# Banks, order and gates in the end phase of a perceiver layer

## The chip, the cores and the metric

The kernel runs on one core of one Trainium2 chip. The time is the device time of the whole program in microseconds, the median of several executions. The program has 70,354 instructions in the profile before.

## The reference, cut to what matters

There are 16 sequences of 128 rows and 512 columns, and each of the three parts adds its result to x:

```python
x = x + xattn(layernorm(x), ctx)      # 16 heads, 2048 context rows for each sequence
x = x + attn(layernorm(x))            # a state-space layer, then an MLP, see below
x = x + ffn(layernorm(x))

# attn, for Z = layernorm(x):
Z_mam = rmsnorm(mamba(Z) + Z) * norm1_w            # in_proj, conv, scan over 128 steps, out_proj
h     = gelu(Z_mam @ mlp_w1.T + mlp_b1)            # 512 -> 2048, the "first matrix"
mlp   = h @ mlp_w2.T + mlp_b2                      # 2048 -> 512, the "second matrix"
attn  = rmsnorm(mlp + Z_mam) * norm1_w

# ffn, for xf = layernorm(x):
scores = softmax(xf @ W_gate)                      # 7 columns, the "gate"
w      = top-2 of scores, divided by their sum
ffn    = xf @ W_shared.T + (sum of w) * (xf @ W_expert.T) + bias   # no token is over capacity here
```

All is in fp32.

## The kernel before

**Stages.** The program is written out in steps u = 0 to 313, in an order set by hand; each engine executes its own instructions strictly in that order and waits for the others by semaphores. For u below 256 (NU, "live") attention fills TensorE. The scan of the state-space layer follows 54 steps behind: each step has two halves, each with ScalarE's decays (L656), VectorE's scan (L670) and product with C (L673) and GpSimd's products and sums (L635, L686). The scan's data bc come by DMA two loads a step (L584).

**The end phase** begins at u = 256, at about 3130 us. Attention's memory is given up and the pool `ffn` opened. The 16 sequences now pass in 8 pairs m = 0 to 7 (i = 0, 1 in a pair) through the MLP and the last part, while the scans of the last sequences still run (until about 3705 us). The work is cut into units, each a list of loads, of TensorE calls, of calls that follow (`post`) and of extra loads. `feed(k)` issues the loads of unit k+2, the extra loads of unit k+1, the post calls of unit k-1 and then the TensorE calls of unit k. Units are dealt out evenly over the steps u; those left after the last step follow without a pause. A pair has:

- four `hidden` units (L829): quarter q of the first matrix, 2 x 16 profile records of 256 columns into two PSUM banks; post: `gelus` (ScalarE, L843, between two table loads), which reads both banks. With quarter 3 go the transposes of the pair before (`x_turned`, L802, and VectorE's copies fT, L813);
- two `expert` units of the pair before (L960): for each sequence 8 records with wex and 8 with wsh, 512 columns each, into a bank each. The first has the `gate` of both sequences ahead (L917, 16 records of 7 columns, one bank). Post: `gated` (softmax and top two, a chain of small VectorE operations, L931 to L951) and `result` (L973 with pe of wex, L976 with psh of wsh, then the output transfer, L977);
- four `second` units (L859): 16 records each, into two banks (`accs`) that are held over all four; post of the last: `mlp_sum` (L877 and moments), and in the next pair's first two quarters `mlp_norm` (L890, L893) and `last_norm` (L906 makes xf; GpSimd adds fbias, L909).

Records: a matmul of fp32 is two records in the profile, each with its own weight load (PEld).

**Banks.** PSUM has eight banks of 512 columns: banks[0] to [3], avp, pa, hst and pc. In the end phase hst and pc hold the scan. `bank()` deals out banks[0], banks[1], avp and pa in a ring of four; each hidden unit 0 of a pair skips two. banks[2] and banks[3] serve the late work of the state-space layer alone: its in_proj (`x_part` and `z_part`, L518, read by ScalarE L528 and VectorE L533), dt (L602, read by ScalarE L606 and VectorE L609), x_proj (L572), the products that turn and scale attention's results (L451, L464, L511) and out_proj (`projected`, L699, read by VectorE L708). The names in the profile: `bank` is any of banks[0] to [3].

**Loads.** All of the loads named here go through SyncE's queue (SP) in program order: weights `wf` (L763, L766; 6 buffers, that is three units), bc (L584), wout (L496), `xr` (L780, the pair's rows, 4 buffers) and x1 (L785).

**The last pair.** Pair 7 has `turn_unit`, its four hidden units, the experts of pair 6, its four second units, and then in one list, for each i: `mlp_sum`, `mlp_norm`, `last_norm`; and for each i: `x_turned`, `gate`, `experts`, `gated`, `result`.

Of the kernel before, what the change touches and what calls it, by code (L numbers as in the profile page):

```python
# [8 lines left out]
FP = mybir.dt.float32  # L9
# [6 lines left out]
P = 128  # L16
# [18 lines left out]
def perceiver_layer(ctx: ExitStack, tc: tile.TileContext, a: dict, out: bass.AP):  # L35
# [28 lines left out]
    def moments(pool, dst, src):  # L64
        st = pool.tile([P, 6], FP, tag="st", name="st", bufs=4)
        nc.vector.bn_stats(st, src)
        nc.vector.bn_aggr(dst, st)
# [41 lines left out]
    with ExitStack() as es:  # L109
# [31 lines left out]
        def heads(ps):  # L141
            return ps.rearrange("p (k q) -> p k q", q=P)
# [572 lines left out]


        fpool, fcs, xrs, hss, mTs, fTs, accs, stage, done = [], {}, {}, {}, {}, {}, {}, {}, set()
        wfs, turn_of = {}, [0]

        def open_ffn():  # L720
            p = es.enter_context(tc.tile_pool(name="ffn", bufs=1))
# [24 lines left out]
        def flat(ps):  # L746
            return ps.rearrange("p k q -> p (k q)")

        def bank():
            t = (banks[0], banks[1], flat(avp), flat(pa))[turn_of[0] % 4]  # L750
            turn_of[0] += 1
            return t

        def seqs(m):
            return [(i, m * MB + i) for i in range(MB)]
# [17 lines left out]
        def load_z(m):  # L773
            for i, b in seqs(m):
                assert b in done
                if m:
                    xrs[b] = fpool[0].tile([P, D], FP, tag="xr", name=f"xr{b}", bufs=4)
                else:
                    xrs[b] = keep.tile([P, D], FP, tag="x", name=f"xr{b}", bufs=4)
                nc.sync.dma_start(xrs[b], zd[b])  # L780
# [24 lines left out]
        def x_turned(m, ii):  # L805

            for i in ii:
                b = m * MB + i
                turned_in(stage.pop((b, "xf")), b, "fT")
            for i in ii:  # L810
                b = m * MB + i
                fTs[b] = fpool[0].tile([P, KC, NQ], FP, tag=f"fT{i}", name=f"fT{b}")
                nc.vector.tensor_copy(fTs[b], heads(stage.pop((b, "fT"))))  # L813

        def turned_pair(m):
            t = fpool[0].tile([P, KC, MT], FP, tag="mT", name=f"mT{m}")
            mTs[m] = t
            for i, b in seqs(m):
                copy = nc.vector.tensor_copy if i else nc.scalar.copy
                copy(t[:, :, i * NQ : (i + 1) * NQ], heads(stage.pop((b, "mT"))))  # L820

        def hidden(m, q):
            if q == 0:
                turn_of[0] += 2
            ps = [bank(), bank()]
            for j in range(4):
                w = wfs[m, 1, q, j // 2]
                for kc in range(KC):
                    nc.tensor.matmul(  # L829
                        ps[j // 2][:, j % 2 * MT : (j % 2 + 1) * MT],  # L830
                        w[:, kc, j % 2 * P : (j % 2 + 1) * P],
                        mTs[m][:, kc, :],
                        start=(kc == 0),
                        stop=(kc == KC - 1),
                    )
            stage[m, q] = ps

        def gelus(m, q):
            ps = stage.pop((m, q))
            t = fpool[0].tile([P, 4, MT], FP, tag="hs", name=f"hs{m}_{q}", bufs=4)  # L840
            for j in range(4):
                fc = q * 4 + j
                nc.scalar.activation(  # L843
                    t[:, j, :],
                    ps[j // 2][:, j % 2 * MT : (j % 2 + 1) * MT],
                    AF.Gelu,
                    bias=fcs["b1"][:, fc : fc + 1],
                )
            nc.scalar.preload_act_table_set("natural_log_exp_and_others")
            hss[m, q] = t  # L850

        def second(m, q):
# [18 lines left out]
        def mlp_sum(m, ii):  # L871

            n = len(ii)
            mv2, r, ms = small("mv2", [P, n, 2]), small("r2", [P, n]), small("ms", [P, n])
            for j, i in enumerate(ii):
                x = xrs[m * MB + i]
                nc.vector.tensor_tensor(x, x, accs[m][i], ALU.add)  # L877
                moments(keep, mv2[:, j, :], x)
            mean_square(keep, ms, mv2)
            inv_sqrt(keep, r, ms, 1e-6)  # L880
            stage[m, *ii, "r2"] = r
# [27 lines left out]
                nc.gpsimd.tensor_tensor(xrs[b], xrs[b], fcs["fbias"], ALU.add)  # L909
                stage[b, "xf"] = xf  # L910

        def gate(m, ii):
            n = len(ii)
            ps = bank()[:, 0 : n * 8].rearrange("p (i e) -> p i e", e=8)[:, :, 0:NE]
            for j, i in enumerate(ii):
                for kc in range(KC):
                    nc.tensor.matmul(  # L917
                        ps[:, j, :],
                        fTs[m * MB + i][:, kc, :],
                        fcs["wg"][:, kc, :],  # L920
                        start=(kc == 0),
                        stop=(kc == KC - 1),
                    )
            stage[m, *ii, "g"] = ps

        def gated(m, ii):

            n, pg = len(ii), stage.pop((m, *ii, "g"))
            gm, gs = small("gm", [P, n, 1]), small("gs", [P, n, 1])
            sc, top = small("sc", [P, n, 8]), small("top", [P, n, 8])  # L930
            nc.vector.tensor_reduce(gm, pg, AX.X, ALU.max)  # L931
            nc.vector.memset(sc, 0.0)
            nc.vector.tensor_tensor(
                sc[:, :, 0:NE], pg, gm.to_broadcast([P, n, NE]), ALU.subtract
            )
            nc.scalar.activation(sc[:, :, 0:NE], sc[:, :, 0:NE], AF.Exp)
            nc.vector.tensor_reduce(gs, sc[:, :, 0:NE], AX.X, ALU.add)
            nc.vector.reciprocal(gs, gs)
            nc.vector.tensor_tensor(
                sc[:, :, 0:NE], sc[:, :, 0:NE], gs.to_broadcast([P, n, NE]), ALU.mult  # L940
            )
            for j in range(n):
                nc.vector.max(top[:, j, :], sc[:, j, :])
            nc.vector.tensor_tensor(gs, top[:, :, 0:1], top[:, :, 1:2], ALU.add)
            nc.vector.reciprocal(gs, gs)
            nc.vector.tensor_tensor(
                top[:, :, 0:2], top[:, :, 0:2], gs.to_broadcast([P, n, 2]), ALU.mult
            )


            nc.vector.tensor_tensor(gs, top[:, :, 0:1], top[:, :, 1:2], ALU.add)  # L951
            for j, i in enumerate(ii):
                stage[m * MB + i, "gs"] = gs[:, j, :]

        def experts(m, i):
            b = m * MB + i
            ps = [bank(), bank()]
            for t, w in zip(ps, (fcs["wex"], fcs["wsh"])):
                for kc in range(KC):
                    nc.tensor.matmul(  # L960
                        t,
                        fTs[b][:, kc, :],
                        w[:, kc, :],
                        start=(kc == 0),
                        stop=(kc == KC - 1),
                    )
            stage[b, "e"] = ps

        def result(m, i):
            b = m * MB + i  # L970
            pe, psh = stage.pop((b, "e"))
            r = flat_tile(f"res{b}")
            nc.vector.scalar_tensor_tensor(  # L973
                r, pe, stage.pop((b, "gs")), xrs[b], ALU.mult, ALU.add
            )
            nc.vector.tensor_tensor(r, r, psh, ALU.add)  # L976
            nc.sync.dma_start(out[b], r)  # L977


# [3 lines left out]
        def unit(loads=(), pe=(), post=()):  # L983
            units.append(([*loads], [*pe], [*post], []))
# [19 lines left out]
                units[-1][1].insert(0, call(x_turned, m - 1, both))  # L1004

        def expert_units(m):
            for i in range(MB):
                unit((), [call(experts, m, i)], [call(result, m, i)])
            units[-2][1].insert(0, call(gate, m, both))
            units[-2][2].insert(0, call(gated, m, both))  # L1010

        def second_units(m):
            for q in range(4):
# [35 lines left out]
        turn_unit(m, ())  # L1049
        units[-1][1].pop(0)  # L1050
        hidden_units(m)
        expert_units(m - 1)
        second_units(m)
        for i in both:
            units[-1][1].extend(call(f, m, (i,)) for f in (mlp_sum, mlp_norm, last_norm))
        for i in both:
            units[-1][1].extend([call(x_turned, m, (i,)), call(gate, m, (i,))])
            units[-1][1].extend([call(experts, m, i), call(gated, m, (i,)), call(result, m, i)])


        late, after, inner, middle, loads, head, behind = ({} for _ in range(7))
# [94 lines left out]
        for u in range(last):  # L1156
# [26 lines left out]
                weighted(u - 1)  # L1183
            if u == NU:
                att.close()
                open_ffn()
            if u == NU + 8:
                load_wex()
# [31 lines left out]
            for f in middle.get(u, ()):  # L1220
                f()
            for i, f in enumerate(after_turns):
                f(banks[(3 + i) % 4 if live else 2 + i % 2])
            if live and after_turns:
                turn(u, 3, (3 + len(after_turns)) % 4)
            for f in behind.get(u, ()):
                f(pc.rearrange("p k q -> p (k q)") if makes else banks[2])
            for f in after.get(u, ()):
                f()
            for f in inner.get(u, ()):  # L1230
# [81 lines left out]
```

## Time and profile before

| | |
|---|---|
| median of three runs | 3881.88 us (3880.52 to 3889.77) |
| the profiled execution | 3884.85 us |
| its span, first to last instruction | 3883.1 us |
| granted TensorE clock, mean | 0.986 |
| busy share of PE, DVE, ACT, POOL | 97%, 70%, 63%, 54% |
| PE busy in 3140 to 3724 us (584 us) | 539.0 us |
| DVE, ACT, POOL busy there | 399.8, 279.6, 370.2 us |

PE is TensorE's matmuls, PEld its weight loads, DVE VectorE, ACT ScalarE, POOL GpSimd, SP SyncE; L829 is line 829 of the kernel before. In a timeline a row gives its start, its length, the engine, line and operation, output<-inputs, shape, the number of instructions in it, and in brackets the idle time ahead of it and what ended that. In the waits a row gives who waited for whom, the sum in us, the number of waits and the longest. A row of stretches gives the stretch, its length, the busy time and count of PE, PEld, DVE, ACT and POOL, the granted TensorE clock (1.00 is full), the DMA engines' busy share and GB/s. The ends of matmuls are modelled, so their pace is read from start to start.

### The profile page before, as it was taken

How to read it: one execution, taken by the hardware profiler on the slowest of the kernel's cores; microseconds unless marked ns; L12 is line 12 of the kernel's file. 1: busy time of each engine (PE TensorE's matmuls, PEld its weight loads, DVE VectorE, ACT ScalarE, POOL GpSimd, SP SyncE). 2: the span in 40 equal slices, each digit the busy share in tenths (PEclk: the TensorE clock that was granted, in tenths of full speed). 3: DMA queues.
4: the chain of work that ended last, by engine and by line, in shares of the span. 5: the costliest groups of instructions: out<-in, count | busy, mean ns of one | idle time of the engine just before them, and what ended most of it. 6: DMA issues, size and time to landing. Idle time of an engine off the chain costs nothing.

```text
span 3883.1 us, 70354 instructions
## 1 busy us (share of the span) xinstructions
PE 3771.4 (97%) x26120; PEld 2868.8 (74%) x26120; DVE 2713.3 (70%) x4852; ACT 2445.5 (63%) x5847; POOL 2104.8 (54%) x1968
## 2 busy tenths in 40 slices
PE   7999999999999999999999999999999989899998
PEld 6888787778777877787778777877787756555654
DVE  3444445887778787878787878787878776758732
ACT  3555556777767776777677767776777654434421
POOL 1111113675667566756676657665766575657710
PEclk9999999999999999999999999999999999999999
DMA  2111122444444444444445354435353477567641
GB/s 91 42 34 44 50 71 78 139 148 136 140 161 147 144 140 159 143 149 137 161 138 157 124 167 146 152 118 177 130 162 121 153 261 237 180 230 239 227 157 59
DMA packets 341223, 548.40 MB, mean 141 GB/s; under 512 B 24432, under 2 KB 225408, under 8 KB 340624
## 3 DMA queue, kind: packets, MB, share of 16 engines
q1 hardware_dynamic: 340464, 543.28, 42.6%
q8 instruction: 206, 3.38, 0.4%
q14 instruction: 137, 1.12, 0.1%
q0 software_dynamic: 416, 0.63, 0.1%
HBM read 527.29 MB, written 16.52 MB: 140 GB/s over the span
## 4 chain that ended last, share of the span: by engine, by line
PE 81%; DVE 10%; ACT 4%; issue 2%; DMA 2%; POOL 1%; SPq 0%; DVEq 0%; ACTq 0%; POOLq 0%
PE pa L237 21%; PE pc L237 15%; PE bank L330 10%; PE bank L299 7%; PE bank L518 6%; PE avp L343 6%; PE bank L699 3%; DVE hst L670 2%; DVE nm L307 2%; PE bank L859 2%; DVE w L673 2%; PE bank L395 2%; PE bank L464 2%; PE bank L960 1%; PE bank L829 1%
## 5 line engine op out<-in xcount | busy, mean ns | idle before, releaser
L307 DVE TENSOR_REDUCE nm<-bank 128x1 f32<-128x512 f32 x1024 | 634.9, 682 | 251.3 <-PE bank L299 250.3
L686 POOL TENSOR_TENSOR ysum<-ysum,w 128x512 f32<-128x512 f32 x384 | 500.5, 1303 | 500.5 <-DVE hst L649 303.3
L317 ACT ACTIVATE pr<-bank,nm 128x512 f32<-128x512 f32 x1024 | 689.7, 687 | 95.0 <-DVE nm L307 89.2
L635 POOL TENSOR_TENSOR w<-dx,bc 128x512 f32<-128x512 f32 x512 | 649.5, 1290 | 3.8
L335 ACT COPY pT<-bank 128x512 f32<-128x512 f32 x816 | 437.6, 585 | 222.0 <-PE bank L330 217.9
L670 DVE TENSOR_TENSOR_SCAN hst<-hst,w 128x512 f32<-128x512 f32 x456 | 556.9, 1221 | 11.9 <-ACT hst L656 8.1
L656 ACT ACTIVATE hst<-dt,alog 128x254 f32<-128x254 f32 x912 | 436.4, 478 | 169.0 <-DVE hst L649 150.5
L330 PE MATMUL bank<-ident,pr 128*128 128x128 f32 x4096 | 525.4, 275 | 16.2 <-ACT pr L317 14.3
L330 PEld LDWEIGHTS bank<-ident,pr 128*128 128x128 f32 x4096 | 472.0, 142 | 74.6 <-ACT pr L317 22.2
L343 PEld LDWEIGHTS avp<-pT,v 128*32 128x32 f32 x8192 | 208.0, 109 | 193.9 <-issue 193.9
L673 DVE TENSOR_TENSOR w<-hst,bc 128x512 f32<-128x512 f32 x456 | 315.3, 692 | 47.8 <-DMA bc<-bcd 32.4
L299 PE MATMUL bank<-kt,qT 32*128 32x512 f32 x2048 | 297.7, 642 | 6.1 <-DVE avs L458 5.7
L229 POOL TENSOR_TENSOR t<-c,c 128x512 f32<-128x512 f32 x128 | 164.8, 1288 | 252.3 <-PE pc L237 244.7
L343 PE MATMUL avp<-pT,v 128*32 128x128 f32 x8192 | 276.8, 276 | 0.0
L237 PE MATMUL pa<-t,ks 128*128 128x256 f32 x1024 | 249.3, 386 | 0.0
L237 PE MATMUL pa<-vs,t 128*128 128x256 f32 x1008 | 244.7, 386 | 0.0
L518 PE MATMUL bank<-zT,win 128*128 128x256 f32 x1024 | 234.6, 383 | 4.6 <-ACT hs L843 4.6
L518 PEld LDWEIGHTS bank<-zT,win 128*128 128x128 f32 x1024 | 192.0, 192 | 30.9 <-ACT hs L843 5.0
L237 PEld LDWEIGHTS pa<-vs,t 128*128 128x128 f32 x1008 | 185.4, 190 | 34.6 <-issue 10.1
L317 ACT ACTIVATION_READ_ACCUMULATOR pr<-bank,nm 128x1 f32 x1024 | 209.6, 205 | 0.0
L237 PEld LDWEIGHTS pa<-t,ks 128*128 128x128 f32 x1024 | 185.1, 190 | 32.7 <-issue 10.3
L333 DVE COPY pT<-bank 128x512 f32<-128x512 f32 x208 | 143.8, 691 | 89.1 <-PE bank L330 86.5
(274 smaller groups left out, 6849.4 us busy)
## 6 DMA issues: line engine op xcount, KB each, us to landing
bc<-bcd SPq DMA_DIRECT2D x512, 512.0 KB, 4.3
c<-in_ctxT_dram SPq DMA_DIRECT2D x256, 256.0 KB, 4.4
wf<-in_w_dram SPq DMA_DIRECT2D x128, 512.0 KB, 7.3
wqo<-in_wqkvo_dram SPq DMA_DIRECT2D x128, 256.0 KB, 4.8
win<-in_win_dram SPq DMA_DIRECT2D x128, 256.0 KB, 4.6
wout<-in_wout_dram SPq DMA_DIRECT2D x128, 256.0 KB, 4.3
x<-in_x_dram SPq DMA_DIRECT2D x16, 256.0 KB, 3.6
x1d<-x SPq DMA_DIRECT2D x16, 256.0 KB, 2.2
```

Source lines behind the costliest of these rows:

```text
L237: nc.tensor.matmul(ps[:, r, :], l[:, kc, r * P : (r + 1) * P], m[:, kc, :], start=(i in (1, 2, 5) and r == 0 and kc == 0), stop=(r == 1 an ...
L299: nc.tensor.matmul(banks[j], qts[b][rows, hg, :], kts[u // 4, hg][rows, :], start=True, stop=True)
L307: nc.vector.tensor_reduce(stats[b][0][j][:, sb, hg : hg + 1], banks[j], AX.X, ALU.max, negate=True)
L317: nc.scalar.activation(pr[:, j, :], banks[j], AF.Exp, bias=nm[j][:, sb, hg : hg + 1], accum_out=sm[:, sb, h : h + 1],)
L330: nc.tensor.transpose(ps[:, j, :], prs[u][:, j, i * P : (i + 1) * P], ident)
L335: nc.scalar.copy(pT, ps)
L343: nc.tensor.matmul(avp[j * HD : (j + 1) * HD, hg, :], vts[u // 4, hg // 2, i // 2][:, i % 2, hg % 2 * P + j * HD : hg % 2 * P + (j + 1) * HD],
L518: nc.tensor.matmul(ps, w[:, kc, :], zTs[g][:, kc, :], start=(kc == 0), stop=(kc == KC - 1))
L635: nc.gpsimd.tensor_tensor(w, dx.unsqueeze(1).to_broadcast([P, NH // 2, GT]), bcs[g * 32 + r, 0][:, i * NH // 2 : (i + 1) * NH // 2, :], AL ...
L656: nc.scalar.activation(bt(h[:, k, :])[:, :, 1:], bt(dt)[:, :, 1:], AF.Exp, scale=aneg[:, ec, n : n + 1],)
L670: nc.vector.tensor_tensor_scan(flat, flat, w.rearrange("p n t -> p (n t)"), 0.0, ALU.mult, ALU.add)
L686: nc.gpsimd.tensor_tensor(s, s, w, ALU.add)
```

## The change

- `bank()` takes the oldest entry of a list, `free_banks`; six banks are put into it at u = 256 (pa, banks[2], banks[1], avp, and banks[3] and banks[0] after `turned_pair`), and each reader gives its bank back where it is issued. The late work takes its banks from the same list.
- `xr` has 6 buffers instead of 4.
- `gate` is gone: in `experts` each chunk's gate matmul follows the wex matmul on the same fT chunk. `gated` comes after both experts; `result` is split: first xr + psh, later, in `result_last`, + gs x pe, and the output transfer.
- For the last pair the second units, with `mlp_sum`, `mlp_norm` and `last_norm`, come ahead of the experts of pair 6; `x_turned` of each sequence of pair 7 stands after an expert unit of pair 6; then follow the two expert units of pair 7.

```diff
         def bank():
-            t = (banks[0], banks[1], flat(avp), flat(pa))[turn_of[0] % 4]
-            turn_of[0] += 1
-            return t
+            return free_banks.pop(0)
+
+        def give_back(*ps):
+            free_banks.extend(ps)
...
-                    xrs[b] = fpool[0].tile([P, D], FP, tag="xr", name=f"xr{b}", bufs=4)
+                    xrs[b] = fpool[0].tile([P, D], FP, tag="xr", name=f"xr{b}", bufs=6)
...
-                nc.vector.tensor_copy(fTs[b], heads(stage.pop((b, "fT"))))
+                ps = stage.pop((b, "fT"))
+                nc.vector.tensor_copy(fTs[b], heads(ps))
+                give_back(ps)
...
         def hidden(m, q):
-            if q == 0:
-                turn_of[0] += 2
             ps = [bank(), bank()]
...
             nc.scalar.preload_act_table_set("natural_log_exp_and_others")
+            give_back(*ps)
             hss[m, q] = t
...
                 nc.vector.tensor_tensor(x, x, accs[m][i], ALU.add)
+                give_back(accs[m][i])
...
-        def experts(m, i):
-            b = m * MB + i
+        def experts(m, ii, j):
+
+            b = m * MB + ii[j]
+            if j == 0:
+                stage[m, *ii, "g"] = bank()
+            pg = stage[m, *ii, "g"][:, j * 8 : j * 8 + NE]
             ps = [bank(), bank()]
-            for t, w in zip(ps, (fcs["wex"], fcs["wsh"])):
+            for t, w in zip(ps, ("wex", "wsh")):
                 for kc in range(KC):
-                    nc.tensor.matmul(
-                        t,
-                        fTs[b][:, kc, :],
-                        w[:, kc, :],
-                        start=(kc == 0),
-                        stop=(kc == KC - 1),
-                    )
+                    for o, x in ((t, w), (pg, "wg"))[: 2 if w == "wex" else 1]:
+                        nc.tensor.matmul(
+                            o,
+                            fTs[b][:, kc, :],
+                            fcs[x][:, kc, :],
+                            start=(kc == 0),
+                            stop=(kc == KC - 1),
+                        )
             stage[b, "e"] = ps
 
         def result(m, i):
             b = m * MB + i
-            pe, psh = stage.pop((b, "e"))
+            pe, psh = stage[b, "e"]
             r = flat_tile(f"res{b}")
-            nc.vector.scalar_tensor_tensor(
-                r, pe, stage.pop((b, "gs")), xrs[b], ALU.mult, ALU.add
-            )
-            nc.vector.tensor_tensor(r, r, psh, ALU.add)
+            nc.vector.tensor_tensor(r, xrs[b], psh, ALU.add)
+            give_back(psh)
+            stage[b, "e"] = pe, r
+
+        def result_last(m, i):
+            b = m * MB + i
+            pe, r = stage.pop((b, "e"))
+            nc.vector.scalar_tensor_tensor(r, pe, stage.pop((b, "gs")), r, ALU.mult, ALU.add)
+            give_back(pe)
             nc.sync.dma_start(out[b], r)
...
         def expert_units(m):
-            for i in range(MB):
-                unit((), [call(experts, m, i)], [call(result, m, i)])
-            units[-2][1].insert(0, call(gate, m, both))
-            units[-2][2].insert(0, call(gated, m, both))
+            for i in both:
+                unit((), [call(experts, m, both, i)], [call(result, m, i)])
+            units[-1][2].append(call(gated, m, both))
+            units[-1][2].extend(call(result_last, m, i) for i in both)
...
         hidden_units(m)
-        expert_units(m - 1)
         second_units(m)
         for i in both:
             units[-1][1].extend(call(f, m, (i,)) for f in (mlp_sum, mlp_norm, last_norm))
+        expert_units(m - 1)
+        units[-1][1].insert(0, call(x_turned, m, (0,)))
+        units[-1][1].append(call(x_turned, m, (1,)))
         for i in both:
-            units[-1][1].extend([call(x_turned, m, (i,)), call(gate, m, (i,))])
-            units[-1][1].extend([call(experts, m, i), call(gated, m, (i,)), call(result, m, i)])
+            unit(
+                (),
+                [call(experts, m, (i,), 0)],
+                [call(f, m, x) for f, x in ((gated, (i,)), (result, i), (result_last, i))],
+            )
...
             if u == NU:
                 att.close()
+                give_back(flat(pa), banks[2], banks[1], flat(avp))
                 open_ffn()
...
             for i, f in enumerate(after_turns):
-                f(banks[(3 + i) % 4 if live else 2 + i % 2])
+                ps = banks[(3 + i) % 4] if live else bank()
+                f(ps)
+                if not live:
+                    give_back(ps)
...
             for f in behind.get(u, ()):
-                f(pc.rearrange("p k q -> p (k q)") if makes else banks[2])
+                ps = flat(pc) if makes else banks[2] if live else bank()
+                f(ps)
+                if not live:
+                    give_back(ps)
```

## The prediction

> **What bounds the kernel now.** I read the page first, then the waits of PE in the end phase (3120 us to the end), then PE's timeline around the longest of them, the timeline of SP's queue, the last 40 us, and last the stretches of DVE. The page says where to look:
>
> ```profile
> PE 3771.4 (97%) x26120; PEld 2868.8 (74%) x26120; DVE 2713.3 (70%) x4852; ACT 2445.5 (63%) x5847; POOL 2104.8 (54%) x1968
> ...
> PE   7999999999999999999999999999999989899998
> ```
>
> Over the span of 3883.1 us PE is the bound, and what it loses it loses at the end: the last eight slices are the end phase, the only part that the change touches. Its waits there:
>
> ```profile
> PE bank L829 <- ACT hs L843: 12.7, 3, 4.7
> PE bank L917 <- DVE fT L813: 8.1, 2, 7.2
> PE bank L859 <- DMA wf<-in_w_dram: 6.5, 1, 6.5
> ...
> PE pa L829 <- ACT hs L843: 5.8, 1, 5.8
> PE avp L829 <- ACT hs L843: 5.4, 1, 5.4
> ```
>
> Three causes: the first matrix (L829) waiting for gelus to empty a bank, 23.9 us; a weight transfer, 6.5 us; the tail's chain (L917 and L802), 8.1 us here and 4.5 of L802. (A wait of L518 for L533's reads, 4.6 us in pair 1, stays as it is.) A wait costs more than its length. In pair 3:
>
> ```profile
> 3443.78 3.62 PE L829 MATMUL pa<-mT,wf 128*128 128x256 f32 x16
> 3447.23 0.59 PE L602 MATMUL bank<-xd,dtw 128*128 128x256 f32 x2
> 3447.66 1.28 PE L802 MATMUL bank<-ident,xf 128*128 128x128 f32 x8
> 3454.35 6.20 PE L829 MATMUL avp<-mT,wf 128*128 128x256 f32 x16 [5.41 <-ACT hs L843]
> 3460.39 3.62 PE L829 MATMUL pa<-mT,wf 128*128 128x256 f32 x16
> ```
>
> Sixteen records take 3.45 us from start to start at full clock (3443.78 to 3447.23) and 6.04 us after the wait (3454.35 to 3460.39): a wait of 5.41 us also costs 2.6 us of half clock.
>
> **Part 1, the banks.** The ring of four gives the last quarter of the first matrix the very banks of the quarter before it, because the two transposes of the other pair took the two in between. So PE waits there until gelus has read them. Such waits stand in pairs 1, 3, 4, 5 and 6: 3.83 + 5.41 + 5.81 + 4.67 + 4.16 = 23.9 us, and the matmuls behind them run 1.8, 2.6, 2.1, 2.0 and 3.1 us over their full-clock pace: 11.5 us. Together 35.4 us. With six banks in one line the order of the changed program puts that quarter into banks of the quarter before the last, of the dt product (L602), or of an x or z product; none waits for the newest gelus.
>
> What is late next? (a) The quarter's second half then reuses L602's bank in pairs 3 and 4. L602 ended at 3447.66 and DVE's read of it (L609) at 3453.02: 5.4 us. PE comes back to the bank after 0.87 us of transposes and 3.45 us of matmuls, 4.3 us: a wait of 1.1 us. (b) The first expert product takes a bank that the newest gelus must free. In pair 3 gelus ended 7.8 us after its matmuls (3455.03 against 3447.23); PE is back after 0.43 + 0.87 + 6.9 = 8.2 us: none, just. (c) In pair 1, expert product and second matrix take banks that an x product (L518) left 1.7 to 2.2 us before. L602 sits in that place now and waits 0.5 us: two such, bounds 0 to 5 us, I take 2. (d) The last projection's DVE read stands 0.9 us ahead of the second matrix of pair 6; DVE idles there (9.41 us busy in the 50 us from 3700), so 0.2 us.
>
> Against all this stands DVE:
>
> ```profile
> 3500.00:3600.00 100.00, 93.90 (x330) 60.38 (x329) 80.83 (x157) 49.86 (x105) 73.88 (x70) 0.97 0.69 236
> 3600.00:3700.00 100.00, 88.99 (x324) 59.40 (x323) 76.98 (x146) 51.50 (x102) 68.47 (x60) 0.96 0.71 242
> ```
>
> ```profile
> DVE w L673 <- DMA bc<-bcd: 11.7, 3, 5.1
> ```
>
> Two stretches of 100 us, then DVE's waits from 3500 to 3700. DVE's busy time is the third of a stretch's: 79%, and another 12% of these 200 us it waits for something other than PE (11.7 for bc, 7.6 for ACT's decays, 5 of small ones). A pair takes 82 us there (3508.79 to 3590.57 for pair 4). DVE so needs about 75 us, 70 if the DMA waits go; PE's matmuls at full clock need 73: four quarters 27.6, second matrix 27.5, experts with gates 15.4, transposes and a dt product 2.2. The removed stalls cannot all be won with the engines so close and each in order. I let 3 us a pair come back as short waits in the five pairs, 15 us; bounds 0 and, if DVE is the bound, all 35.
>
> A clock question hangs on those short waits. In this trace a wait of 3.01 us (L572 for POOL, 3344.00) was followed by half clock: four transposes took 0.91 us instead of 0.44, and in all 2.6 us were lost; waits of 1.80 us and less were not. The Trainium skill ("TensorE: Matmul & The Clock Gate", Part 1) has the clock halve only after an idle window of about 3.4 us. By the page, short waits cost their length; by the row, one of 3 us nearly doubles. If all five did, that would be 13 us more.
>
> **Part 2, six xr buffers.** SP's queue in pair 2:
>
> ```profile
> 3372.59 5.84 SPq L780 DMA_DIRECT2D xr<-zd  x2
> ...
> 3386.77 0.99 SPq L766 DMA_DIRECT2D wf<-in_w_dram  x2
> ```
>
> SP stands from 3363 on: the reload of xr waits until the results of the pair two back have been read out of its buffer (3372.57 and 3378.09), and everything behind it on SP stands too: bc, wout and the weights wf, for some 15 us. PE then waits 1.1 + 6.5 us for wf and loses another 2.9 us to half clock: the 48 records from 3372.61 plus the 1.27 us ahead of them came to 10.5 us over pace. With six buffers the owner was done a pair earlier. The weights come up to 15 us earlier than a wait of 6.5 needs: I count all 10.5 us as gone, bounds 0 and 10.5.
>
> **Part 3, gates.** Sixteen sequences times 8 records at 0.1065 us (16 in 1.70 us, 3463.84 to 3465.55) are 13.6 us in both kernels. Interleaved, the first gate record of a chunk hides its weight load behind a 512-column matmul; the second and the next expert matmul show theirs: two a chunk, eight a sequence, as now. Cost 0; bounds 13.6 less (loads skipped) and 13.6 more (each switch showing one more). No row has such a switch; the nearest, 128-column transposes, also come at 0.107 a record. The Trainium skill ("TensorE: Matmul & The Clock Gate", "Back-to-back issue gap") gives a matmul of up to 64 columns a floor of 25 ns; by that the gates would shrink by 128 x 0.08 = 10 us, an estimate from the page that enters no sum. The top-two chain and the product with pe move behind both experts; DVE does them while PE is in the second matrix, but its later result holds the gate bank and two expert banks longer, which the six banks cover.
>
> **Part 4, the tail.**
>
> ```profile
> 3841.93 3.60 PE L859 MATMUL avp<-wf,hs 128*128 128x512 f32 x8
> 3850.04 1.12 PE L802 MATMUL pa<-ident,xf 128*128 128x128 f32 x4 [4.52 <-DVE xf L906]
> 3858.34 1.87 PE L917 MATMUL bank<-wg,fT 128*128 128x7 f32 x8 [7.17 <-DVE fT L813]
> ...
> 3871.30 1.06 PE L917 MATMUL bank<-wg,fT 128*128 128x7 f32 x8 [0.94 <-DVE fT L813]
> ```
>
> From the end of the first accumulator (3841.93) to the end of the span are 41.2 us now, and pair 6's experts took another 15.5 us before the second matrix (3802.37 to 3817.89): 56.7. Changed: second accumulator 3.43; four expert blocks of 3.43 + 0.86 + 3.43 = 7.72; two transposes of 0.43; and one new wait, since the first expert block of pair 7 takes the bank of the transposes just ahead of it and must await DVE's copy, 0.94 as in the last row. That is 36.1 us. Then DVE: 0.2 + 0.69 for psh and now 0.79 for pe after it, and 3.05 us of output transfer (3880.05 to 3883.1 now). Sum 40.9; gain 15.8. DVE's two chains (3842.20 to 3857.68) end 15.7 us after that start; PE first wants their second result at 3.43 + 7.72 + 0.43 + 7.72 = 19.3 us. Cover 3.6 us; past it, each us of DVE delay costs one.
>
> The weights for the second matrix follow straight on the first's; the first matrix already streams four quarters unbroken from 3777, with loads two units ahead, and SP's order puts pair 6's output transfers behind all of them instead of between. POOL, past which pair 7's additions of fbias move, is idle from 3800.
>
> **Sum.** Banks 35.4 - 15 - 2; transfer 10.5; tail 15.8: 44.7 us off the profiled execution's 3884.85 gives 3840.2. The median of the runs, 3881.88, lies 3.0 below that execution: 3837.
>
> **Rivals.**
> (A) The stalls only change owner: DVE's 75 us and in-order queues hold the pairs, and the tail alone is won: 3881.9 - 16 = 3866. For it: 79% plus 12%. Against: DVE itself waited 11 us on late gates and 16 us on the projections between 3400 and 3700, waits that an earlier PE ends.
> (B) Nothing comes back: 35.4 + 10.5 + 15.8 = 62 off, 3820. For it: (a), (b) and (d) are each about a microsecond.
> (C) Slower: banks whose reader is DVE stand close behind their writer in the new line. If DVE trails PE so that each of six pairs waits w more, plus 2.6 us half clock, the 62 us are eaten when 6(w + 2.6) = 62, w = 7.7 us; at w = 12 it is 3908. Against: L609's 5.4 us is what DVE trails now.
> (D) No change: each gate switch shows one more weight load (13.6 us), and the stalls change owner as in (A): 3880.
>
> **Numbers.** Forecast 0.52, A 0.20, B 0.16, C 0.07, D 0.05. Range 3818 to 3868: just past B and just past A. Some 0.3%, 12 us, is what a measurement can tell from no change: faster 0.88 (forecast, A, B), same 0.05 (D), slower 0.07 (C).
>
> **What would show it.** Right: no wait of the first matrix for gelus over 2 us in pairs 3 to 6; no half clock between them; no xr reload standing on SP; PE unbroken from the second matrix of pair 7 to its last product but for about 1 us; gates at 0.21 us a chunk. Wrong: PE waits on L609 or L533 banks of over 3 us; DVE over 90% busy from 3500; PE waiting for scans at the projections; 512-column matmuls off their 0.43 us pace beside gates.

## The result, and the profile after

The changed kernel takes 3821.44 us (median; 3821.10 to 3821.82) against 3882.53 us for the kernel before, measured beside it: 61 us less, a ratio of 0.9839 with a 95% interval of 0.9822 to 0.9856. The profiled execution took 3821.10 us, its span 3819.3.

The predicted time was 3837, so 15.6 us too long. The time lies beside rival B, "nothing comes back", at 3820. All of the profile after has the line numbers of the changed kernel: the first matrix is L834 (L829 before), the second L865 (L859), transposes of x L805 (L802), their copies L817 (L813), xf L913 (L906), experts and gates L960.

The page first, its head, the line of engines and PE's slices:

```profile
span 3819.3 us, 70341 instructions
...
PE 3747.7 (98%) x26120; PEld 2856.3 (75%) x26120; DVE 2711.8 (71%) x4852; ACT 2445.3 (64%) x5847; POOL 2104.1 (55%) x1968
...
PE   7999999999999999999999999999999989999999
```

Three of the last eight slices were at 8 before, one is now, that in which the end phase begins. The waits of PE from 3120 us to the end, all that are 0.5 us or longer:

```profile
PE pa L834 <- DMA wf<-in_w_dram: 7.3, 1, 7.3
PE bank L518 <- ACT hs L848: 4.6, 1, 4.6
PE bank L834 <- issue: 3.9, 1, 3.9
PE bank L572 <- POOL xa L566: 3.0, 1, 3.0
PE avp L805 <- DVE xf L913: 2.8, 1, 2.8
PE avp L699 <- DMA wout<-in_wout_dram: 1.8, 1, 1.8
PE bank L330 <- ACT pr L317: 1.7, 4, 0.7
PE bank L960 <- DVE fT L817: 0.8, 1, 0.8
PE bank L834 <- DVE dt L609: 0.7, 1, 0.7
PE avp L602 <- ACT zs L547: 0.5, 1, 0.5
PE bank L865 <- ACT zs L547: 0.5, 1, 0.5
```

The first matrix no longer waits for a gelu anywhere (23.9 us before), the second no longer for weights (6.5), and the tail's 12.6 us of waits have become 0.8. What is left was there before, but for the line of L834 on L609 (0.7), which the prediction had at 1.1. Three waits have grown: 2.8 us for xf in pair 5 (1.8 at the same place before), 7.3 for the first weights of the phase (6.0) and 1.8 for wout (0.8). The 4.6 us of L518 are the wait for L533's reads that the prediction names: the last of these ends at 3227.53 us and L518 starts at 3227.63, while the view puts the wait down to a gelu. In pair 3, where the timeline before had a wait of 5.41 us and half clock:

```profile
3427.33 0.59 PE L602 MATMUL bank<-xd,dtw 128*128 128x256 f32 x2
3427.76 1.28 PE L805 MATMUL bank<-ident,xf 128*128 128x128 f32 x8
3428.88 3.62 PE L834 MATMUL bank<-mT,wf 128*128 128x256 f32 x16
3433.17 3.72 PE L834 MATMUL bank<-mT,wf 128*128 128x256 f32 x16 [0.67 <-DVE dt L609]
3436.73 1.02 PE L960 MATMUL avp<-wex,fT 128*128 128x512 f32 x2
```

From start to start the quarter's halves take 4.29 us with the wait and 3.56 us, against 3.45 at full pace; no gelu is waited for, and the clock stays full.

SP's queue in pair 2, in which the reload of xr stood before:

```profile
3365.83 0.49 SPq L597 DMA_DIRECT2D dtw<-in_dtproj_dram  x1
3367.04 0.95 SPq L769 DMA_DIRECT2D wf<-in_w_dram  x2
3368.39 1.03 SPq L982 DMA_DIRECT2D out_dram<-res  x2
3369.68 1.20 SPq L584 DMA_DIRECT2D bc<-bcd  x2
```

Weights, results and bc follow each other with no xr among them; pair 3's rows were loaded earlier. VectorE over the same two stretches of 100 us as before (its busy time is the third of each stretch):

```profile
3500.00:3600.00 100.00, 97.06 (x352) 62.96 (x350) 83.58 (x148) 61.12 (x122) 81.76 (x75) 0.98 0.68 227
3600.00:3700.00 100.00, 100.00 (x324) 58.35 (x323) 58.06 (x127) 33.63 (x67) 49.15 (x43) 1.00 0.69 242
```

It is busier in the first (83.6 against 80.8) and far less busy in the second (58.1 against 77.0): the scans are done sooner, the last starts at 3659.8 us and not at 3702.2. The tail:

```profile
3778.15 3.60 PE L865 MATMUL avp<-wf,hs 128*128 128x512 f32 x8
...
3797.54 0.60 PE L805 MATMUL bank<-ident,xf 128*128 128x128 f32 x4
3798.92 1.13 PE L960 MATMUL bank<-wex,fT 128*128 128x512 f32 x2 [0.78 <-DVE fT L817]
3799.89 0.28 PE L960 MATMUL pa<-wg,fT 128*128 128x7 f32 x2
3800.03 1.10 PE L960 MATMUL bank<-wex,fT 128*128 128x512 f32 x2
...
3811.03 3.68 PE L960 MATMUL bank<-wsh,fT 128*128 128x512 f32 x8
```

From the second accumulator's start (3778.15) to the end of the span are 41.15 us; the prediction's sum was 40.9.

**Where the time went.** For every TensorE record of the end phase I took the time from its start to the next one's start, less what such a record takes at full clock without a wait (0.429 us for 512 columns, 0.215 for 256, 0.1075 for 128, 0.1065 for a gate's 7). That is the time over pace: waits and half clock together. In both kernels the records at full pace come to 645 us. Over pace, in three sections: from the first matrix's first record until the second out_proj of the phase has passed (pairs 0 to 2), from there to the transposes of pair 7 (pairs 3 to 6), and from these to the end.

| profiled execution | pairs 0 to 2 | pairs 3 to 6 | pair 7 and tail |
|---|---|---|---|
| before | 40.2 | 35.2 | 24.8 |
| predicted for the change | 29 | 17 | 8 |
| changed | 19.2 | 7.0 | 8.3 |

The predicted row is the one before, less the prediction's gains by place. First section: pair 1's wait with its half clock, 5.6, and the transfer, 10.5, less 3 + 2 given back. Second: four waits of 20.1 us with 9.8 of half clock, less 4 x 3. Third: 15.8, and the 0.8 us that VectorE's later product adds behind PE's end. The two excesses of 10 us, less the 1.2 us by which the end phase began later (3134.46 against 3133.26), are the 19 us by which the profiled execution beat the sum (3821.1 against 3840.2). The tail has no part in it.

### The profile page after: what moved, and what is told of

It reads as the page before. It is cut to its first block, busy times and chain, and to the rows that moved or that the text cites. A ratio compares the mean times of both kernels' runs of the same rounds, so it can differ in the third digit from the quotient of the medians.

```text
span 3819.3 us, 70341 instructions
## 1 busy us (share of the span) xinstructions
PE 3747.7 (98%) x26120; PEld 2856.3 (75%) x26120; DVE 2711.8 (71%) x4852; ACT 2445.3 (64%) x5847; POOL 2104.1 (55%) x1968
## 4 chain that ended last, share of the span: by engine, by line
PE 84%; DVE 9%; ACT 3%; issue 2%; DMA 1%; POOL 1%; SPq 0%; DVEq 0%; ACTq 0%; POOLq 0%
PE pa L237 21%; PE pc L237 15%; PE bank L330 10%; PE bank L299 7%; PE avp L343 6%; PE bank L518 5%; PE bank L865 3%; PE bank L699 3%; DVE hst L670 2%; PE bank L834 2%; PE bank L960 2%; DVE nm L307 2%; PE bank L395 2%; DVE w L673 2%; PE bank L464 1%
## 5 line engine op out<-in xcount | busy, mean ns | idle before, releaser
L518 PE MATMUL bank<-zT,win 128*128 128x256 f32 x968 | 222.0, 383 | 4.6 <-ACT hs L848 4.6
L237 PEld LDWEIGHTS pa<-t,ks 128*128 128x128 f32 x1024 | 184.7, 190 | 32.6 <-issue 10.5
L518 PEld LDWEIGHTS bank<-zT,win 128*128 128x128 f32 x968 | 181.5, 192 | 28.7 <-ACT hs L848 5.0
```

Of the source, the lines that this page charges most:

```text
L237: nc.tensor.matmul(ps[:, r, :], l[:, kc, r * P : (r + 1) * P], m[:, kc, :], start=(i in (1, 2, 5) and r == 0 and kc == 0), stop=(r == 1 an ...
L518: nc.tensor.matmul(ps, w[:, kc, :], zTs[g][:, kc, :], start=(kc == 0), stop=(kc == KC - 1))
```

## The experiments

Theory N: the removed stalls stay away, because six xr buffers also free the data that VectorE waits for. Theory G, the prediction's: VectorE is so near its limit that some 3 us a pair come back. All kernels are compared with the kernel before, run on the same chip (medians 3880.3, 3881.2 and 3880.4 us for the three sets below).

### The parts one by one

Six xr buffers in the kernel before, nothing else:

```diff
-  xrs[b] = fpool[0].tile([P, D], FP, tag="xr", name=f"xr{b}", bufs=4)
+  xrs[b] = fpool[0].tile([P, D], FP, tag="xr", name=f"xr{b}", bufs=6)
```

> The kernel before with six xr buffers, nothing else. Both theories take the reload of xr off SP's queue in pair 2. Theory N (nothing comes back): the 10.5 us of the late weights go, 3871, and VectorE's waits for bc (11.7 us from 3500 to 3700) fall below 2 us; the waits of the first matrix on gelus stay, 24 us in all. Theory G (VectorE gives the rest back, as predicted): the same 10.5, since this term holds none of the give-back. A rival: the late weights were only hidden behind the next wait, 3876 to 3882.

Measured 3867.77 us, ratio 0.9969 (0.9957 to 0.9980): 12.5 off. The second matrix's wait for wf in pair 2 fell from 6.5 to 0.9 us. VectorE's waits for bc fell from 32.4 to 9.4 us over the end phase, and from 3500 to 3700 none is left among its waits. The waits for gelus stayed (21.5 us). The term of 10.5 us holds.

The banks alone: `bank()`, `give_back` and every place that gives a bank back as in the change, on the kernel before.

```diff
-            t = (banks[0], banks[1], flat(avp), flat(pa))[turn_of[0] % 4]
-            turn_of[0] += 1
-            return t
+            return free_banks.pop(0)
...
-            if q == 0:
-                turn_of[0] += 2
...
+            give_back(*ps)
```

> The kernel before with the six banks in one line alone: four xr buffers, gates ahead of the expert matmuls, the old order of the tail. Theory N (short waits do not come back): 35.4 us go, 3847. Theory G (3 us a pair come back as short waits, and 2 for the banks of L518): 3864. A third, theory S: the stalls do come back here, because TensorE reaches the reload of xr earlier and SP then stands longer, and only six xr buffers keep them away: 3858 or more, with waits for wf or bc of over 10 us in pairs 2 to 6.

Measured 3854.63 us, ratio 0.9934 (0.9922 to 0.9947): 25.7 off, of 35.4, by the medians 9.7 us less than the sum and between N and S. The execution that was profiled, 3848.96 us, is the fastest of the five, so its trace shows where time came back rather than how much of these 9.7 us.

The same with six xr buffers:

> The kernel before with six banks in one line and six xr buffers; gates and tail as before. Theory N: 35.4 + 10.5 = 46 us off, 3836, so that gates and tail are worth the other 15 us. Theory G: 28 off, 3853, and what the changed kernel gained beyond that came from the interleaved gates. Theory S: 3836 as N, but more than the sum of the two parts alone.

Measured 3836.05 us, ratio 0.9888 (0.9873 to 0.9903): 44.2 off, of 45.9. Now next to nothing comes back. The parts alone sum to 38.2; the 6 us between are no larger than the intervals allow by chance, so the traces must say where they are. VectorE's waits for bc from 3330 to 3690 us, in the kernel before, with the banks alone and with both:

```profile
DVE w L673 <- DMA bc<-bcd: 25.6, 7, 5.1
```

```profile
DVE w L673 <- DMA bc<-bcd: 27.4, 9, 6.3
```

```profile
DVE w L673 <- DMA bc<-bcd: 9.0, 5, 4.2
```

(0.3 us with the buffers alone, 1.4 in the changed kernel.) So four buffers keep these waits as they were, and six remove most of them, with the old banks as with the new. Where VectorE stands behind the reload, TensorE can stand behind VectorE. One such place with the banks alone, PE's timeline in pair 3:

```profile
3480.75 1.02 PE L863 MATMUL bank<-wf,hs 128*128 128x512 f32 x2
3483.61 0.65 PE L803 MATMUL pa<-ident,xr 128*128 128x128 f32 x4 [1.84 <-DVE xr L796]
3484.27 1.06 PE L803 MATMUL bank<-ident,xr 128*128 128x128 f32 x4
3485.13 4.92 PE L863 MATMUL avp<-wf,hs 128*128 128x512 f32 x8
```

The wait for the next pair's rows (z_norm, which VectorE reaches late) costs 2.0 us and, with the half clock until 3487.8, another 2.0 (1.3 of it in the last row). The sections, over pace, in one execution each:

| profiled execution | pairs 0 to 2 | pairs 3 to 6 | pair 7 and tail |
|---|---|---|---|
| before, 3884.85 us | 40.2 | 35.2 | 24.8 |
| buffers alone, 3867.92 us | 28.3 | 29.2 | 24.2 |
| banks alone, 3848.96 us | 27.8 | 12.8 | 23.0 |
| both, 3835.92 us | 20.9 | 4.7 | 24.6 |

The 29.9 us of stalls removed in pairs 3 to 6 would leave 5.3 of the 35.2: so 7.5 came back without the buffers and none with them. But the buffers alone took 6.0 us off these pairs, where the prediction counted nothing for them (among them shorter gelu waits, 5.17 us instead of 5.81 in pair 4 and 2.35 instead of 4.16 in pair 6). There the parts alone sum to 6.0 + 22.4 = 28.4 us and both took 30.5: most of it is what each is worth by itself, and that one helps the other beyond this, by 2 us here and 6 by the medians, is not shown beyond the noise.

The new order of the last pair alone, on the kernel before (gates apart, the ring of four banks):

```diff
         hidden_units(m)
-        expert_units(m - 1)
         second_units(m)
...
+        expert_units(m - 1)
+        units[-1][1].insert(0, call(x_turned, m, (0,)))
+        units[-1][1].append(call(x_turned, m, (1,)))
```

> The kernel before with the new order of the last pair alone: pair 7's second matrix ahead of pair 6's experts, its transposes around the second of these; old ring of banks, four xr buffers, gates ahead of the experts. Both theories: 15.8 us off, 3866, and TensorE's waits for L906 and L813 after 3800 fall from 12.6 us to about 1. If the ring of four makes the experts wait for banks: 3868 to 3872.

Measured 3870.61 us (3866.08 to 3876.23), ratio 0.9976 (0.9968 to 0.9985): 9.7 off, not 15.8. The ring is why, in PE's timeline:

```profile
3834.26 0.60 PE L802 MATMUL bank<-ident,xf 128*128 128x128 f32 x4
3838.30 6.59 PE L960 MATMUL avp<-wex,fT 128*128 128x512 f32 x8 [3.44 <-DVE sc L933]
```

The second expert block gets the bank in which pair 6's gates lie, and VectorE reaches these only behind pair 7's two norms: 3.4 us of wait and 3.0 of half clock. On top of banks and buffers the same order, with the interleaved gates, took the span from 3834.1 to 3819.3 us: 14.8. So the tail's gain needs the six banks, which the prediction had not seen.

### The gates

The changed kernel with the gate records as a block ahead of the expert records of each sequence:

```diff
-            for t, w in zip(ps, ("wex", "wsh")):
+            for t, w in zip((pg, *ps), ("wg", "wex", "wsh")):
```

> The changed kernel with the 8 gate records of a sequence ahead of its 16 expert records, as a block, instead of one after each chunk of wex. Prediction's term (cost 0): 3821, within 2 us. If interleaving saved weight loads or issue gaps: up to 13.6 us slower, 3835. If each switch between gate and expert chunk cost something: up to 13.6 us faster, 3808. A place where it can cost by another way: the tail's two last blocks, where the gate's results come 3 us earlier here, which is off the path that ends the kernel.

Measured 3819.48 us, ratio 0.9841 (0.9827 to 0.9854), against 0.9839: no difference. A sequence in pair 3:

```profile
3438.82 0.95 PE L959 MATMUL pa<-wg,fT 128*128 128x7 f32 x8
3439.63 3.68 PE L959 MATMUL avp<-wex,fT 128*128 128x512 f32 x8
3443.15 3.60 PE L959 MATMUL bank<-wsh,fT 128*128 128x512 f32 x8
3446.58 0.95 PE L959 MATMUL pa<-wg,fT 128*128 128x7 f32 x8
```

3438.82 to 3446.58 are 7.76 us. Interleaved, in the tail, 3781.58 to 3789.34 are 7.76 too. The term of 0 was right, and a gate record costs 0.11 us either way (a chunk of wex takes 1.08 us with its gate, 0.86 without). The floor of 25 ns for narrow matmuls in the Trainium skill ("TensorE: Matmul & The Clock Gate", "Back-to-back issue gap"), which would have given 10 us, is not reached in either order.

### How near is VectorE to its limit?

Idle VectorE work behind each gelu call of pairs 1 to 6, on a tile of its own:

```diff
             hss[m, q] = t
+            if 1 <= m <= 6:
...
+                for _ in range(4):
+                    nc.vector.tensor_tensor(spare[0], spare[0], spare[0], ALU.min)
```

> The changed kernel with four idle VectorE operations (128x256, about 0.4 us each, on a tile that nobody else uses) added behind each gelu call of pairs 1 to 6: 24 calls, about 6 us more of VectorE work a pair, 38 us in all. The outputs are not touched. Theory G (VectorE needs about 70 us of a pair's 73 to 75): 2 to 3 us a pair come onto the path, 3835. Theory N (VectorE has a quarter of its time free, 148 us of the 550 from 3140 to 3690, and its idle time can be used): 3821 to 3824.

> The same with ten operations a call, about 15 us more of VectorE work a pair, 90 us in all, the outputs again untouched. Theory G: 11 to 12 us a pair, 3890. Theory N: the 148 us of idle time take nearly all of it; with 27 us free a pair against 15 added, 3825 to 3835 from single late results.

Then, with one operation a call:

> The changed kernel with one idle VectorE operation (128x256) behind each gelu call of pairs 1 to 6, 24 in all; outputs untouched. The two larger loads put 79.5 us of such work (0.83 us each, not the 0.4 expected) onto VectorE for 31 us of time, and 156.7 us (0.65 each) for 98. Theory R (room, then one for one: 50 to 60 us in six pairs are free, some 9 a pair): 24 x 0.8 = 20 us fit in, 3821 to 3824. Theory P (each us of VectorE work costs 0.4 us from the first on): 8 us, 3829.

The added groups, for four operations a call and for ten (count, busy us, mean ns):

```profile
L862 DVE TENSOR_TENSOR spare<-spare 128x256 f32<-128x256 f32 x96 | 79.5, 828 | 2.8
```

```profile
L862 DVE TENSOR_TENSOR spare<-spare 128x256 f32<-128x256 f32 x240 | 156.7, 653 | 7.7
```

| added VectorE work | time | over the changed kernel's 3821.4 | over pace, all three sections |
|---|---|---|---|
| none | 3821.4 | | 34.5 |
| 20.2 us | 3829.4, ratio 0.9867 (0.9850 to 0.9883) | +8.0 | 41.4 |
| 79.5 us | 3852.5, ratio 0.9926 (0.9914 to 0.9939) | +31.0 | 67.4 |
| 156.7 us | 3919.1, ratio 1.0099 (1.0086 to 1.0113) | +97.7 | 131.4 |

Both theories fall here. N said that idle time (148 of 550 us) takes the load; I had then supposed 50 to 60 us of room (R). There is none: each us of VectorE's work costs about 0.4 us of time from the first on (P; 0.34 by the trace of the first load), and over 0.8 between the last two rows. A rival, that the added work slows GpSimd and GpSimd the rest, is not it: GpSimd's instructions took 389.6 us in all in the end phase without load and 392 to 394 with. G's floor of 70 us a pair falls as well, since below a floor work costs nothing. VectorE is free a quarter of the time and yet on the path for part of what it does; the chains for which TensorE stands in line in these traces (z_norm, last_norm, the reads of dt) are the likely places. By this price the 18.4 us that bc waits fell from 27.4 to 9.0 are worth 0.4 x 18.4 = 7.4 us (an estimate); over pace in pairs 3 to 6 fell by 8.1.

### Towards a better version

The trace after shows 3.94 us of wait and 2.9 us of half clock at pair 7's first quarter, 2.80 us and as much half clock again as makes 4.4 in pair 5, and 0.95 us in the tail. First all three at once: the last unit of pair 6 dealt behind the last scan step with pair 7's transposes ahead of it, the transposes of x moved into the middle of the quarter, and the scans' two banks in line:

```diff
-        feeds = len(units) - 1
+        feeds = len(units) - 2
...
+            else:
+                units[-2][1].insert(0, call(z_norm, m + 1))
...
+                if between and j == 2:
+                    between(two)
...
+        give_back(flat(hst), flat(pc))
```

> The changed kernel with three places mended that its trace still shows: pair 7's z_norm, transposes and copies stand ahead of the last quarter of pair 6's second matrix, as in the other pairs (the wait of 3.94 us and 3.1 us of half clock behind it, 7.0); the two transposes of x in the middle of the first matrix's last quarter instead of ahead of it (a wait of 2.80 us for L913 and what half clock follows, 4.5 in pair 5); the two banks of the finished scans join the line for the tail (0.95). If each mends its own and nothing comes back: 12 us off, 3809. If the earlier last projection must wait for the scans: VectorE's last scan was done 22 us ahead of it, so 6.9 us earlier costs nothing; if it does, 3813 to 3816. A rival: the shifted order moves a stall elsewhere, 3819 or more.

Measured 3830.46 us, ratio 0.9869 (0.9855 to 0.9882): 9 us slower than the changed kernel, the rival. Pair 7 and the tail fell to 0.2 us over pace, all 8 won; pairs 0 to 2 rose from 19.2 to 28.9, pairs 3 to 6 from 7.0 to 12.5. A wait for a gelu is back:

```profile
3590.08 6.19 PE L838 MATMUL bank<-mT,wf 128*128 128x256 f32 x16 [4.12 <-ACT hs L852]
```

Which edit did it? The same without the split:

> As second_step but without moving the transposes into the middle of the first matrix's last quarter: the last quarter of pair 6's second matrix is dealt behind the last scan step, pair 7's transposes ahead of it, the scans' banks join the tail. If the moved transposes brought second_step its new waits on gelus (6.7 us) : 3813. If the dealing of one unit fewer over the 57 steps did, since every unit then meets other late work and other banks: 3828 or more.

Measured 3829.41 us, ratio 0.9866 (0.9851 to 0.9881); over pace 27.1, 14.2 and 0.2. The dealing did it: ahead of pair 6's second matrix nothing else differs from the changed kernel. That each unit then stands beside other late work is the expected reason; it is not shown place by place.

Now the tail's edits without touching the dealing:

```diff
-            if m < NF - 1:
+            if m < NF - 2:
                 units[-1][2].append(call(mlp_sum, m, both))
...
+        units[-1][2].append(call(mlp_sum, m - 1, both))
...
+        give_back(flat(hst), flat(pc))
```

> The changed kernel with two edits behind 3700 us: mlp_sum of pair 6 stands behind the copies of pair 7's transposes, and the banks of the finished scans join the line for the tail. Nothing ahead of 3700 moves. The wait of 3.94 us for the copy falls to about 1 us (a copy of 0.68 behind the transposes), and the 2.9 us of half clock go if a wait of 1 us leaves the clock alone: 6 off; the 0.95 us in the tail goes: 3814.5. Rival: mlp_sum, now 4 us later, holds the second matrix's banks and delays pair 6's own rows, which the tail has room for: no cost. If the wait only moves to the first gelus or banks: 3819 to 3821.

Measured 3812.97 us (3811.58 to 3815.60), ratio 0.9825 (0.9810 to 0.9839), the fastest of all. Its interval overlaps that of the changed kernel, so the gain rests on the trace: 20.1, 7.4 and 1.3 us over pace, 7.0 less in the last section and no gain elsewhere. The end phase of this execution also began 3.8 us earlier (3130.64 against 3134.46), which no edit behind 3700 us can cause: the trace gives the edits 6 to 7 us of the 8.5 between the medians. The place itself:

```profile
3715.23 0.60 PE L805 MATMUL bank<-ident,xn 128*128 128x128 f32 x4
3715.67 0.60 PE L805 MATMUL avp<-ident,xn 128*128 128x128 f32 x4
3717.10 7.14 PE L834 MATMUL bank<-mT,wf 128*128 128x256 f32 x32 [0.83 <-ACT mT L826]
```

The copies of the transposes no longer queue behind mlp_sum on VectorE: 0.83 us instead of 3.94, and 32 records in 6.98 us (to 3724.08), full clock.

The same with the split:

> As late_sum, with the two transposes of x in the middle of the first matrix's last quarter. Where the split is harmless and second_step lost by its dealing: the wait of 2.80 us for L913 in pair 5 and its half clock go as well, 3810. Where the split is at fault: 3820 to 3826.

Measured 3814.68 us (3813.18 to 3818.28), ratio 0.9830 (0.9815 to 0.9844): no gain; over pace 25.1, 5.2 and 1.3. The wait for xf is gone and others stand in its place, in PE's waits:

```profile
PE bank L838 <- ACT hs L852: 2.6, 2, 2.3
PE bank L838 <- ACT hst L656: 2.1, 1, 2.1
```

Neither expected value (3810 or 3820 and more) came; the split moves a stall of 2.8 us rather than ends it.

## Why the prediction was right, and where it was not

- **Part 1, what is removed: right.** All five waits of the last quarter for gelus are gone, with their half clock.
- **Part 1, what is late next: (a) to (d) nearly right.** L609's bank costs 0.67 us where 1.1 stood; the first expert product waits for no gelu; beside the x and z products stand two waits of 0.5, as many as before, where the sum had 2 us more; L708 costs nothing visible.
- **Part 1, the give-back of 15 us: the term that failed, with the 2 of (c).** It was put at 3 us in each of five pairs, and in pairs 3 to 6 the runs show 7.5 of these 12 us with four xr buffers (the banks alone) and none with six. These 4.5 us and the 6.0 that the buffers alone are worth there, which Part 2 put at nothing, are the 10 us by which pairs 3 to 6 beat the sum. The prediction knew that VectorE's need falls "if the DMA waits go" and that bc stands behind xr on SP; but it costed the buffers by pair 2 alone and charged the banks for a delay that the buffers remove. Its picture of a floor (70 or 75 us a pair) was wrong too: VectorE has a price, some 0.4 us a us at the two smaller loads and more at the largest.
- **Part 1, smaller:** 4 to 5 us more went in pairs 0 to 2 that no term held. In the kernel before these are a wait of L602 for a bank (0.73, after L451 at 3156.67), 1.75 us of half clock at L960 (3254.65), 0.9 at the start of the phase and 1.6 of the 1.69 at L829 (3346.81). The last two are luck as far as the traces show: the same waits stand ahead of them, and less half clock fell behind (3.5 us of it instead of 5.3 at the start, a stretch of 3.4 instead of 6.8 at L829).
- **Part 2: right in size for the place it was counted at,** 12.5 measured alone for 10.5, and no reload of xr stands on SP; what it left out is the 6.0 us above. One of its two waits was misread: the 1.11 us ahead of the second matrix (3372.61) end with VectorE's read of an expert bank (L973) and not with a weight; they stay with the buffers alone (1.1) and go with the banks alone.
- **Part 3: right,** 0 within the interval, 0.22 us a chunk for 0.21.
- **Part 4: right in size** (41.15 us for 40.9; a wait of 0.78 for 0.94), but only with the six banks; alone it is worth 9.7.
- **The clock:** that waits of 1.80 us and less left it alone was misread. Behind the wait of 0.52 us at 3252.42 the expert products ran at half clock (8 records in 5.19 us, 3254.65 to 3259.84, instead of 3.43); the last section says what lay beside it.
- **The signs:** one failed. Half clock was to be absent between pairs 3 and 6, and came once, behind the 2.80 us for xf at 3578. None of the wrong signs came; VectorE was 84% busy from 3500 to 3600.

So rival B gave the time, and its reason ((a), (b) and (d) small) was sound; the missing piece was that the buffers also free VectorE in pairs 3 to 6.

## What to carry to other kernels

When a change has parts, price each on the state that the others leave: a stall in one in-order queue (here SP behind a buffer's reuse) can be what makes another engine late, far from the place where it shows. An engine with a quarter of its time idle may still cost some 0.4 us for each us of work added, so a busy share gives neither room nor a floor; a small added load measures the price directly. An order that fixed one place (the last unit behind the scans) cost more by shifting all the others; the edit that left the dealing alone kept its gain.

## What the runs showed of the hardware

**The clock halves on a fixed grid.** In each of the 14 traces the changes of the granted clock lie on multiples of 3.413 us from each other, and what a wait costs depends on how it falls on that grid. The windows of the banks alone around the wait of 1.84 us, cut at the grid (granted clock after the five busy times):

```profile
3480.97:3484.38 3.41, 1.56 (x7) 0.53 (x6) 3.27 (x9) 0.88 (x3) 2.04 (x2) 1.00 1.05 374
3484.38:3487.79 3.41, 3.41 (x8) 1.85 (x9) 3.27 (x5) 1.47 (x3) 1.27 (x1) 0.50 0.92 317
3487.79:3492.00 4.21, 4.21 (x11) 1.85 (x10) 4.06 (x8) 1.61 (x4) 3.54 (x5) 1.00 0.82 278
```

TensorE was idle (by the modelled ends of its matmuls) for 1.85 of the first 3.41 us, and the next 3.41 ran at half clock. Over all traces, from 3145 us to the end of TensorE's work, 83 such windows at full clock were followed by half clock: 82 had at least 1.85 us idle, one 0.52. Of those that were not, the idlest had 1.93 us; 48 had between 1 and 1.93. The one is in the kernel before, from 3251.20 us, and holds a block of 16 gate records of 7 columns (L917, 1.7 us). If gate records are counted as idle it has 2.04 us, all 83 have at least 1.85 and of the others still none has over 1.93. The way back is as sharp in this count: 83 windows at half clock with at most 0.54 us idle were followed by full clock, 72 with at least 0.59 were not. So about 1.9 us idle within one window sufficed, not the whole window that the Trainium skill names ("TensorE: Matmul & The Clock Gate", Part 1, an idle window of about 3.4 us): the grid agrees, the share does not. By this reading a single wait of up to 1.8 us is safe if its window holds neither another wait nor a gate block, and a longer one can be if the edge of a window divides it.

**VectorE beside GpSimd.** The added operation reads and writes SBUF alone. It took 0.414 us at least, 0.426 in the median and 1.493 at most in the kernel with ten a call. The 154 of which GpSimd instructions overlapped less than 5% took 0.42 us on average, the 32 that they overlapped by over 95% took 1.18. That is why the first load came to 79.5 us and not 38. An operation with one input in PSUM did not lengthen: L883 in the changed kernel took 0.67 to 0.69 us each, and 11 of its 16 lay wholly beside GpSimd instructions. The Trainium skill ("SBUF — State Buffer", "SBUF: two separate sides") has VectorE and GpSimd share one port pair under an exclusive lock, which fits.
